# Softmax denominators from pairs of key chunks added by an accumulating DMA, and first expert layers beside the last of layer 1

## The chip, the cores and the metric

The kernel runs on one core of one Trainium2 chip. The metric is the device time of a run in microseconds (us). The engines have short names in the profile: PE is TensorE's products, PEld its weight loads, DVE is VectorE, ACT is ScalarE, POOL is GpSimd and SP is SyncE, which here only issues DMAs. A PSUM tile is a buffer that products are written to; an eviction is the ScalarE instruction that reads such a tile and writes its values elsewhere; a DMA's landing is the moment at which the profile sees it done. The granted clock is the share of full speed that the profile gives for TensorE.

## The reference, cut to what matters

```python
# x: 8 images, 256 channels, 32 x 32 pixels, float32
# layer 0: attention over pooled keys and values, 8 heads of 32, 1426 keys
attn = softmax(einsum('bhqd,bhkd->bhqk', q_g, k) * SCALE)
out_att = einsum('bhqk,bhkd->bhqd', attn, v)
...                                # projection, added to x
# layer 1: attention over tokens, then 8 experts on every token
t = t + attn(_ln_t(t))
h = relu(bn(einsum('bfd,edh->bfeh', x, W1) + b1))
h = relu(bn(einsum('bfeh,ehk->bfek', h, W2) + b2))
y = einsum('bfeh,ehd->bfed', h, Wo) + bo
t = t + einsum('bfed,fe->bfd', y, w)   # w: gates from the mean over all images
```

The gates need all eight images, so the experts' third products cannot start before layer 1 has ended for the last one. Their first two layers need only their own image.

## The kernel before

It has three stages: a start (first image's pooled keys and values), the attention loop of layer 0, and the experts. The loop has 8 images x 2 groups of four heads x 2 halves of the queries x 12 key chunks = 384 steps. A step makes the scores of one chunk, the Exp on ScalarE, and for the chunk before it the values and the denominators; the denominators are products with a matrix of ones:

```python
def scores(b, c, sl, kc):
    t = T(psum, [P, 4, 512], "sc")                 # one buffer
    for j in range(4):                             # four heads, row-tiled
        f.pe.matmul(t[:w, j, :], lhsT=ks[b, c][r, k0 : k0 + w], rhs=qs[b, c][r, sl], ...)
    pt = T(work, [P, 4, 512], "pt", bufs=2)
    f.act.activation(pt[:w], t[:w], AF.Exp, scale=SCALE0)

def values(b, c, kc, pt, pv):
    for what in range(2):                          # 0: values, 1: ones
        for j in range(4):                         # column-tiled
            lhsT = kit.ones[:w, :DH] if what else vts[b][kc // 4][:w, kc % 4, h * DH : (h + 1) * DH]
            f.pe.matmul(pv[DH * j : DH * j + DH, what, :], lhsT=lhsT, rhs=pt[:w, j, :], ...)
```

`f` is a recorder. It keeps a simple clock for each engine, holds a list of background jobs (pooling, statistics, projections, layer 1), puts pieces of them between the steps, and pins every engine's instructions in the order in which it wrote them. The experts of the kernel before do not use it; there, the ordering tool that schedules the rest of the program is free:

```python
def layer(dst, wt, e, src, s, c):                  # one expert layer, 256 -> 256, 512 tokens
    ps = T(psum, [P, 2, 512], "sc")                # two buffers
    for m in range(2):
        for k in range(2):
            nc.tensor.matmul(ps[:, m, :], lhsT=wt[:, e, k, m * P : (m + 1) * P], rhs=src[:, k, :], ...)
    for m in range(2):
        nc.scalar.activation(dst[:, m, :], ps[:, m, :], AF.Relu, bias=col(c, e, m), scale=col(s, e, m))
```

## Time and profile before

The median of three runs is 3865.12 us (3863.69 to 3868.33). The profiled execution, from the timeline of TensorE:

| stage | from, to (us) | length |
|---|---|---|
| start, to the first scores | 0 to 177.9 | 177.9 |
| attention loop, 384 steps | 177.9 to 2281.2 | 2103.3 |
| end of layer 1, gates, experts | 2281.2 to 3859.8 | 1578.6 |

Two rows of the page cut the span into 40 slices of 96 us; a digit is the busy share in tenths, of TensorE and of the 16 DMA engines:

```profile
PE   3499999999899899899899997799999999999999
...
DMA  1010001000010010010000010500000000000000
```

TensorE is full nearly everywhere and the DMA engines are nearly empty. The row of groups for the ones products is (busy us, mean ns of one | idle before them):

```profile
L657 PE MATMUL pv<-pt,con 128*32 128x512 f32 (+1 forms) x3072 | 399.7, 592 | 0.0
```

3072 instructions are two for each of four heads in 384 steps. The other views are shown in the prediction.

### The profile page before, as it was taken

To read this page: it belongs to the slowest core of one execution; us is meant where nothing else is said; L and a number is where in the kernel's file an instruction comes from. 1 tells how busy PE (TensorE), PEld (TensorE's weight loads), DVE (VectorE), ACT (ScalarE), POOL (GpSimd) and SP (SyncE) were. 2 spreads that over 40 slices of the span, in tenths; PEclk is the share of its full clock that TensorE was granted. 3 is DMA by queue.
4 is the path that set the end of the run, shared out by engine and by line. 5 is a ranking of instruction groups with operands and counts; after the bars stand their busy time and mean duration, and the time that the engine had idled before them with its cause. 6 is when DMAs were issued, how large, how long until landed. Compare 5 with 4: busy or idle time off the path is not lost.

```text
span 3859.8 us, 40154 instructions
## 1 busy us (share of the span) xinstructions
PE 3625.5 (94%) x16666; PEld 1624.4 (42%) x16666; DVE 1389.2 (36%) x2533; ACT 1505.2 (39%) x1625; POOL 762.8 (20%) x848
## 2 busy tenths in 40 slices
PE   3499999999899899899899997799999999999999
PEld 1233344434444444444444455444444444444444
DVE  5555563846636626636522121211111111111111
ACT  1256555564454554454454421212222222222222
POOL 3132324324224224224222222100000000000000
PEclk7699999999999999999999998879999999999999
DMA  1010001000010010010000010500000000000000
GB/s 40 14 39 26 15 4 47 12 28 20 12 36 20 12 36 23 9 36 23 9 28 28 17 46 23 195 17 17 17 17 16 22 17 28 16 17 17 17 11 12
DMA packets 55296, 99.97 MB, mean 26 GB/s; under 512 B 6448, under 2 KB 31672, under 8 KB 52928
## 3 DMA queue, kind: packets, MB, share of 16 engines
q1 hardware_dynamic: 49440, 84.76, 6.3%
q0 software_dynamic: 1152, 8.39, 0.5%
q10 hardware_dynamic: 4512, 4.16, 0.3%
q8 instruction: 133, 2.18, 0.2%
q14 instruction: 59, 0.48, 0.0%
HBM read 61.64 MB, written 35.66 MB: 25 GB/s over the span
## 4 chain that ended last, share of the span: by engine, by line
PE 75%; DVE 13%; issue 4%; POOL 4%; ACT 4%; DMA 0%; ACTq 0%; POOLq 0%; DVEq 0%
PE sc L1701 23%; PE sm L657 20%; PE y L1748 12%; PE pv L657 11%; DVE acc L657 10%; PE sc L657 8%; ACT pt L657 3%; DVE rec L657 1%; POOL s L657 1%; POOL bound L657 1%; PE y L1743 1%; PE sc L1807 1%; POOL rstd L657 1%; DVE tst L657 0%; POOL acc L657 0%
## 5 line engine op out<-in xcount | busy, mean ns | idle before, releaser
L657 ACT ACTIVATE pt<-sc 128x2048 f32<-128x2048 f32 (+1 forms) x384 | 720.9, 1877 | 547.4 <-PE sc L657 546.8
L1709 ACT ACTIVATE h<-sc,bnvec 128x512 f32<-128x512 f32 x512 | 370.7, 774 | 1011.9 <-PE sc L1701 977.1
L657 DVE SCALAR_TENSOR_TENSOR acc<-p,vec,acc 128x961 f32<-128x961 f32 (+7 forms) x1024 | 628.9, 623 | 150.0 <-POOL acc L657 119.2
L1733 DVE TENSOR_TENSOR h<-h,gb 128x1024 f32<-128x1024 f32 x128 | 156.9, 1225 | 1116.1 <-ACT h L1709 1095.8
L1701 PE MATMUL sc<-hn,w1e 128*128 128x512 f32 x1024 | 462.0, 594 | 9.4 <-DVE bnvec L1676 9.4
L1748 PE MATMUL y<-h,wo 128*128 128x512 f32 x1024 | 463.6, 597 | 0.0
L1701 PE MATMUL sc<-h,w2e 128*128 128x512 f32 x1024 | 460.2, 592 | 0.0
L657 PE MATMUL sc<-q,kn 32*128 32x512 f32 (+1 forms) x3072 | 438.0, 640 | 13.4 <-ACT pt L657 13.3
L657 PE MATMUL pv<-pt,vt 128*32 128x512 f32 (+1 forms) x3072 | 409.9, 605 | 0.0
L657 PE MATMUL pv<-pt,con 128*32 128x512 f32 (+1 forms) x3072 | 399.7, 592 | 0.0
L1701 PEld LDWEIGHTS sc<-hn,w1e 128*128 128x128 f32 x1024 | 195.3, 191 | 255.0 <-issue 255.0
L1748 PEld LDWEIGHTS y<-h,wo 128*128 128x128 f32 x1024 | 194.3, 191 | 251.9 <-issue 251.7
L1701 PEld LDWEIGHTS sc<-h,w2e 128*128 128x128 f32 x1024 | 194.6, 190 | 244.9 <-issue 244.9
L657 PE MATMUL sm<-p,v 128*128 128x256 f32 x1024 | 245.2, 401 | 40.5 <-DVE rec L657 40.5
L657 ACT ACTIVATE p<-sm 128x512 f32<-128x512 f32 (+1 forms) x224 | 130.7, 584 | 364.5 <-PE sm L657 356.4
L657 PE MATMUL sm<-y,t 128*128 128x256 f32 x1024 | 243.3, 387 | 3.1 <-ACT p L657 2.7
L657 PEld LDWEIGHTS sm<-p,v 128*128 128x128 f32 x1024 | 206.7, 203 | 79.5 <-DVE rec L657 42.1
L657 POOL TENSOR_TENSOR rstd<-rstd,mhalf 128x4 f32<-128x4 f32 (+2 forms) x88 | 84.5, 960 | 749.9 <-DVE rstd L657 749.9
L657 PEld LDWEIGHTS sm<-y,t 128*128 128x128 f32 x1024 | 190.5, 191 | 73.5 <-issue 42.6
L657 PEld LDWEIGHTS pv<-pt,con 128*32 128x32 f32 (+1 forms) x3072 | 99.6, 110 | 230.9 <-issue 230.9
L657 PEld LDWEIGHTS sc<-q,kn 32*128 32x128 f32 (+1 forms) x3072 | 115.0, 176 | 193.7 <-issue 119.8
L657 PE MATMUL sm<-xp,kvw 128*128 128x512 f32 (+1 forms) x384 | 176.8, 601 | 15.1 <-DVE xp L657 6.7
(177 smaller groups left out, 2599.3 us busy)
## 6 DMA issues: line engine op xcount, KB each, us to landing
xp<-in_x_dram SPq DMA_DIRECT2D x8, 1024.0 KB, 5.8
t<-in_x_dram SPq DMA_DIRECT2D x8, 1024.0 KB, 6.8
t<-t SPq DMA_DIRECT2D x8, 1024.0 KB, 3.9
res<-t SPq DMA_DIRECT2D x32, 256.0 KB, 3.3
t<-o SPq DMA_DIRECT2D x32, 256.0 KB, 2.4
hn<-o SPq DMA_DIRECT2D x32, 256.0 KB, 2.7
hn<-hn SPq DMA_DIRECT2D x16, 512.0 KB, 4.0
t<-t SPq DMA_DIRECT2D x16, 512.0 KB, 4.0
```

Of the source, the lines that this page charges most:

```text
L657: ins = fn(*args, **kwargs)
L1701: nc.tensor.matmul(ps[:, m, :], lhsT=wt[:, e, k, m * P : (m + 1) * P], rhs=src[:, k, :], start=k == 0, stop=k == 1,)
L1709: nc.scalar.activation(dst[:, m, :], ps[:, m, :], AF.Relu, bias=col(c, e, m), scale=col(s, e, m))
L1733: nc.vector.tensor_tensor(h, h, gb[:, e : e + 1, sl].to_broadcast([P, 2, 512]), ALU.mult)
L1743: nc.tensor.matmul(y[m], lhsT=bo[:, m * P : (m + 1) * P], rhs=gt[:, sl], start=True, stop=False)
L1748: nc.tensor.matmul(y[m], lhsT=wo[:, e, k, m * P : (m + 1) * P], rhs=h[:, k, :], start=False, stop=e == NE - 1 and k == 1,)
L1807: nc.tensor.matmul(ps[:, sl], lhsT=sel[:, e * P : (e + 1) * P], rhs=gt[:, sl], start=True, stop=True)
```

## The change

It has two intents. First, two neighbouring chunks of Exp are added by a DMA that accumulates into the first of them, and one ones product per pair replaces two. Second, the experts' first two layers are written by the same recorder, so that they run beside layer 1 of the last images, staged through DRAM until the gates are known. Much of the recorder and of the buffers changes with it. The core, cut:

```diff
+        def add(kc, pt, into):
+            w = KEY_CHUNKS[kc][1]
+            f.pool.dma_start(out=into[:w]..., in_=pt[:w]..., accum_op=ALU.add)
+
+        def sums(kc, s, total):
+            for j in range(4):
+                f.pe.matmul(total[DH * j : DH * j + DH, :], lhsT=kit.ones[:, :DH], rhs=s[:, j, :],
+                            start=kc == 1, stop=kc == NKC - 1)
...
-            pt = T(work, [P, 4, 512], "pt", bufs=2)
+            pt = T(work, [P, 4, 512], "pt", bufs=6)
...
+                if kc1 % 2:
+                    add(kc1, pts.pop(i - 1), pts[i - 2])
+                    due.append((i + 4, kc1, pts.pop(i - 2), av, behind))   # sums four steps later
...
+        lag = 3.0 if engine == "SP" else LANDING                  # LANDING = 9.5
...
         def layer(dst, wt, e, src, s, c):
-            ps = T(psum, [P, 2, 512], "sc")
+            ps = T(psum, [P, 2, 512], "layer", bufs=2)
             for m in range(2):
                 for k in range(2):
-                    nc.tensor.matmul(
+                    f.pe.matmul(
...
-            for m in range(2):
-                nc.scalar.activation(dst[:, m, :], ps[:, m, :], AF.Relu, ...)
+                f.act.activation(dst[:, m, :], ps[:, m, :], AF.Relu, ...)
+            f.step(PACE2)
...
+        while not gated and n2 < NSTAGED:      # first layers until the gates are there
+            first(n1)
+            n1 += 1
+            if n1 > 1:
+                second(n2, True)               # staged through DRAM
+                n2 += 1
```

## The prediction

> **What bounds the kernel now.** I read the page's busy slices first, to find the stages, then cut the span at the points that the TensorE timeline gives: the first score product starts at 177.9 us, the last at 2281.2, the experts' first product at 2457.5, and from 2552 on TensorE has no gap. The busy time of these stretches (columns: PE, PEld, DVE, ACT, POOL, each with its instructions, then granted clock, DMA share, GB/s):
>
> ```profile
> 0.00:178.00 178.00, 67.32 (x176) 35.06 (x176) 100.72 (x237) 34.42 (x64) 43.90 (x55) 0.70 0.09 29
> 178.00:2282.00 2104.00, 2041.38 (x12822) 888.83 (x12822) 1049.36 (x2025) 1072.99 (x1012) 663.75 (x734) 0.99 0.07 23
> 2282.00:2457.00 175.00, 125.17 (x468) 89.99 (x464) 41.85 (x90) 18.77 (x28) 48.48 (x51) 0.85 0.14 47
> 2457.00:2552.00 95.00, 90.95 (x202) 40.99 (x203) 28.16 (x28) 31.35 (x41) 6.64 (x9) 0.81 0.44 171
> 2552.00:3852.00 1300.00, 1300.00 (x3006) 569.50 (x3006) 168.44 (x152) 347.69 (x481) 0.00 (x0) 1.00 0.05 17
> ```
>
> In the attention loop (384 steps in 2104 us, 5.48 us each) TensorE works 97% of the time; VectorE and ScalarE are at half. So the loop is TensorE's, with 63 us idle. The last image's layer 1 and the gates (2282 to 2552) leave 54 us idle and run at a clock of 0.85 and 0.81. The experts are pure TensorE at full clock. The start is a chain through VectorE. So TensorE work taken out of the loop counts nearly in full, unless something else ends a step later.
>
> What that would be shows in two neighbouring steps without background work:
>
> ```profile
> 1166.00 1.14 PE L657 MATMUL sc<-q,kn 32*128 32x512 f32 x8 [0.20 <-ACT pt L657]
> ...
> 1167.07 1.06 PE L657 MATMUL pv<-pt,vt 128*32 128x512 f32 x8
> 1167.27 1.88 ACT L657 ACTIVATE pt<-sc 128x2048 f32<-128x2048 f32 x1 [1.32 <-PE sc L657]
> ...
> 1167.96 1.04 PE L657 MATMUL pv<-pt,con 128*32 128x512 f32 x8
> ...
> 1169.24 1.14 PE L657 MATMUL sc<-q,kn 32*128 32x512 f32 x8
> ```
>
> The score tile has one buffer, so the next scores wait for this Exp: 1.27 us from the scores' start to the Exp's, 1.88 of Exp, 0.09 to the next scores, 3.24 us in all (1166.00 to 1169.24). TensorE's own starts lie 1.07 (scores), 0.89 (values) and 0.97 (ones) apart, 2.93 in sum. A step with no background is already bound by ScalarE, by 0.2 to 0.3 us.
>
> What ends TensorE's idle time (total, times, longest):
>
> ```profile
> PE sm L657 <- DVE acc L657: 48.9, 4, 18.3
> PE sm L657 <- DVE rec L657: 40.5, 4, 10.3
> PE sm L657 <- POOL diag L657: 21.4, 7, 4.5
> ...
> PE sc L657 <- ACT pt L657: 13.3, 58, 0.6
> ```
>
> The first is the start; the second is one stall of 10 us per image in the middle of the loop, where the written order runs ahead of VectorE; the third is mostly the layer-1 tail.
>
> **What the Trainium skill says.** "TensorEngine Tiling (Array Packing)", Key Properties: changing the tiling mode drains TensorE. The trace agrees: the column-tiled values take 0.89 us when the ones, in the same tiling, follow, and the ones take 0.97 when a full-array product follows. "DMA: Bandwidth & Descriptors", Anatomy of one DMA, gives about 2.0 us plus bytes/436e3 for a DMA issued by GpSimd: 4.4 us for 1 MB, as an estimate. This trace's nearest thing, a plain 1 MB load issued by GpSimd, takes longer to land:
>
> ```profile
> feat<-hn POOLq DMA_DIRECT2D x7, 1024.0 KB, 8.3
> ```
>
> The same page, SDMA does more than copy, puts the largest count for the adding unit at 2048 elements; a row of one Exp tile is 4 x 512 = 2048, so each row can be one piece. No run here shows an accumulating DMA yet. "SBUF — State Buffer", Who interferes with whom, says a DMA does not contend with compute engines, but that GpSimd's descriptor writing can be shut out by VectorE; the trace has GpSimd issues of 0.53 us, too few to test it.
>
> **The change part by part.**
>
> *Ones products.* 384 groups go, 192 come. A removed group costs 0.88: when it goes, the values before it take its drain. Over the loop the spacing has a median of 0.88 (values before ones) and 0.97 (ones before background). A new group stands alone between background and scores: 0.96; directly after the values 0.88. So 384 x 0.88 - 192 x about 0.94 = 338 - 181 = 157 us less TensorE time. The group's busy time (399.7 us, half of it 200) overstates this, because modelled ends overlap and the drain stays.
>
> *Exp becomes the bound of bare steps.* Without ones a bare step has 1.07 + 0.97 = 2.04 us of TensorE work against the 3.24 us of Exp chain, or 3.0 with a sum group. I took the instruction order of both built kernels, gave each background product its spacing from this trace (0.91 us for 512 columns, 0.46 for 256, 0.13 for a transpose), and added up max(0, 3.24 - step). Before: 22 us in 65 steps (the trace has 13 on PE and some more on its weight loads), and a loop of 2038 us against 2041 measured busy, so the count is sound. After: 62 us in 110 steps. So +40 us.
>
> *Shifted background.* The same count gives 898 us of background in the loop before and 782 after: 117 us of layer 1 move behind the loop. That is neutral in work, and it is what the experts' first layers are to run beside.
>
> *Stalls in the loop.* The order is written by a new recording model: it knows the Exp wait, the shared port and open buffers, and no step now has more than 8 us of background. I let the 50 us of stalls other than Exp fall to 30: -20.
>
> *The tail.* Now the first experts' layers alternate with layer 1, staged through DRAM. Idle 54 us. Slow clock: the work between 2282 and 2552 is 106 (layer 1) + 16 layers x 3.43 = 55 + 19 (gates) = 180 us at full clock, against 216 busy, so 36. Of these 90 us I give back 35: the last pair's DMA (about 9 us, with two sum groups directly behind the last values), then reciprocal 3.35 and multiply before the projection, with only one 4 to 8 us batch in between; about 5 us until the first expert weights land; a few short chains. Net -55.
>
> *Start.* The starting value of each depthwise sum moves from GpSimd to ScalarE (saves about 3 us at the first), but the map buffer becomes single and each map waits for the convolution before it (19.4 us each): three gaps of 5 to 7 us more on VectorE, and query products move out of the last 40 us. Net +8.
>
> *Other engines.* ScalarE gains about 74 us (starting values) and 50 (copies with sums), so some 1150 of 1850 us; VectorE gains about 100 (adds of layer 1, attention multiply), about 62% busy. GpSimd loses its sums and gets 192 issues. None becomes a bound on average.
>
> Sum: -157 + 40 - 20 - 55 + 8 = -184 from 3865: about 3680 us. By stages: 186 + 1850 + 1640 + 4.
>
> **The rivals.**
> 1. *The DMA sets the step.* 192 transfers in 1850 us is one per 9.6 us. An accumulate reads two streams and writes one; the page's fit with 2 MB gives 6.8 us, with 3 MB 9.2, and the measured 8.3 us for a plain load hints at more. The sum comes four steps after the issue, 13 us in bare steps and 19 on average, so a landing of 8 to 11 us is hidden. At 12 us of occupancy each the loop would last 2300 us: total near 4130. Against: the changed kernel's own model takes 9.5 us for landing, chosen, I assume, from a measurement. About one in fifteen.
> 2. *The ones come out in full, the Exp wait is filled.* If the background fills what I counted as waiting and the stalls vanish, the loop is 1742 + 10 and the tail loses 80: total near 3560.
> 3. *More stalls.* Several buffers become single, ScalarE's queue delays Exps behind the new evictions, hardware DMAs land later beside accumulates. If the order runs ahead of VectorE as before and 0.2 us per step are added, the loop is 80 us longer: 3760.
>
> **Range and chances.** Rivals 2 and 3 are shifts of -120 and +80 that partly occur; the range is 3590 to 3755. More than 2% faster means below 3788; only rival 1 or a doubled rival 3 misses it.
>
> **What would show it.** Ones products at half the count with about 0.95 us a group; the scores' waits for Exp at 50 to 80 us instead of 13; sums waiting for DMA close to nothing; accumulating DMAs landing in 8 to 11 us; the first scores at about 186 us, the last at about 2035; clock near 1 between there and the experts. It is wrong if sums wait for the DMA in most steps, or if the loop keeps stalls of 10 us per image.

## The result, and the profile after

The changed kernel takes 4093.26 us (median of four runs, 4084.45 to 4096.98), beside 3865.01 for the kernel before. The ratio is 1.0586 (95% interval 1.0567 to 1.0605): slower. A ratio here is the mean time of one kernel's runs over that of the other's runs in the same rounds, so it is not quite the ratio of the medians quoted. Executions over 1.5% slower than the fastest of the same kernel are left out of the means. The prediction, 3680 with a range to 3755, was wrong in sign. By its own stages:

| stage | before | predicted | after | after less predicted |
|---|---|---|---|---|
| start | 177.9 | 186 | 169.8 | -16 |
| loop | 2103.3 | 1850 | 1981.5 | +132 |
| rest | 1578.6 | 1640 | 1931.3 | +291 |

The slices of the kernel after are 102 us each:

```profile
PE   3587899989999989999997889888888888888888
...
DMA  1165645564555455455455211123332000000000
```

Two things differ from before. The DMA engines are half busy through the whole loop, and TensorE has eights all through the experts, where it had nines. The stretches show it in numbers (columns as in the prediction): the loop, the stretch in which experts and layer 1 alternate, and the experts alone:

```profile
170.00:2152.00 1982.00, 1828.00 (x10779) 736.36 (x10778) 1017.14 (x2061) 1148.41 (x1328) 377.57 (x483) 0.97 0.54 119
...
2198.00:2700.00 502.00, 441.04 (x1424) 255.45 (x1424) 113.23 (x227) 146.64 (x234) 21.79 (x28) 0.98 0.24 85
2700.00:4075.00 1375.00, 1198.51 (x2657) 485.37 (x2656) 175.63 (x159) 305.70 (x393) 0.00 (x0) 1.00 0.13 47
```

In the experts alone TensorE is busy 1199 of 1375 us at full clock, where it had no gap before: 176 us are lost there. The waits of TensorE name the releaser (total us, times, longest):

```profile
PE layer L663 <- ACT h L663: 231.5, 256, 2.0
PE sm L663 <- DVE xr L663: 50.9, 16, 6.8
PE sc L663 <- ACT pt L663: 43.3, 65, 1.9
```

256 waits are exactly one for each expert layer (8 experts x 16 half images x 2 layers), 0.90 us each. The timeline shows what such a layer looks like. The kernel before had eight products and then the two evictions as one block:

```profile
2466.35 3.60 PE L1701 MATMUL sc<-h,w2e 128*128 128x512 f32 x8
2466.55 1.45 ACT L1709 ACTIVATE h<-sc,bnvec 128x512 f32<-128x512 f32 x2 [1.66 <-PE sc L1701]
2469.78 3.60 PE L1701 MATMUL sc<-hn,w1e 128*128 128x512 f32 x8
```

After, each layer stops in the middle:

```profile
3501.70 1.88 PE L663 MATMUL layer<-h,w2e 128*128 128x512 f32 x4
3501.90 0.78 ACT L663 ACTIVATE h<-layer,bnvec 128x512 f32<-128x512 f32 x1 [2.08 <-PE layer L663]
3503.62 0.78 ACT L663 ACTIVATE h<-layer,bnvec 128x512 f32<-128x512 f32 x1 [0.94 <-PE layer L663]
3504.45 1.98 PE L663 MATMUL layer<-h,w2e 128*128 128x512 f32 x4 [0.87 <-ACT h L663]
3506.27 3.60 PE L663 MATMUL y<-h,wo 128*128 128x512 f32 x8
```

The second half of the layer (3504.45) waits for the eviction of the first half (3503.62 + 0.78). A layer takes 2.75 + 1.82 = 4.57 us from its start to the next group's, where it took 3.43. That is 1.14 us more, and 256 x 1.14 = 292 us, beside an excess of 291 in the rest of the kernel. (This is one layer, scaled up; over all recorded layers the median is 4.62 us after and 3.43 before.)

In the loop the parts that the prediction counted came. The ones products are half as many and wait for their DMA hardly at all, and a DMA lands in 7.2 us (median):

```profile
L663 PE MATMUL total<-pt,con 128*32 128x512 f32 x1536 | 208.5, 615 | 9.7 <-DMA pt<-pt 9.6
```

```profile
pt<-pt POOLq DMA_DIRECT2D x160, 1024.0 KB, 7.2
```

To see why the loop is nevertheless 132 us too long I added up TensorE's timeline over the loop: each group of products at the spacing that its kind has where nothing waits (1.07 scores, 0.88 a column-tiled group, plus 0.10 where another tiling follows, 0.45 for 512 columns), the waits that the timeline names, and what remains, which is slow clock and small gaps. Later experiments stand in the same table. The count of work is good to some 10 us: f_no_pairs, x_traffic_only, t_copy_only and u_half_traffic run the same products in the same order, and so do a_evict_after and y_no_add, and yet their counts differ by up to 9.

| kernel | loop | work | waits | remainder |
|---|---|---|---|---|
| before | 2103 | 2022 | 62 | 19 |
| after | 1982 | 1761 | 152 | 69 |
| a_evict_after | 1987 | 1753 | 151 | 82 |
| f_no_pairs | 2004 | 1934 | 42 | 28 |
| x_traffic_only | 2116 | 1934 | 129 | 53 |
| t_copy_only | 2048 | 1925 | 74 | 49 |
| u_half_traffic | 2055 | 1929 | 82 | 44 |
| y_no_add | 1868 | 1745 | 75 | 48 |
| z_landing_5p5 | 1910 | 1725 | 120 | 64 |
| w_nopairs_landing | 1915 | 1877 | 24 | 15 |

The work fell by 261 us, near the predicted 157 + 117 = 274. But the waits rose by 90, of which Exp, by the names of the waits, is only 30 (13 to 43), and the remainder by 50. Against the prediction's 1850, stalls other than Exp are 80 us too many (60 more where 20 fewer were expected), the remainder 50, the missing part of the work 13, and Exp 10 too few.

### The profile page after: what moved, and what is told of

It is laid out like the page before. It is cut to its first block, busy times and chain, and to the rows that moved or that the text cites. A ratio compares the mean times of both kernels' runs of the same rounds, so it can differ in the third digit from the quotient of the medians.

```text
span 4082.6 us, 37798 instructions
## 1 busy us (share of the span) xinstructions
PE 3558.1 (87%) x15130; PEld 1525.1 (37%) x15130; DVE 1419.7 (35%) x2701; ACT 1651.0 (40%) x2050; POOL 422.1 (10%) x552
## 5 line engine op out<-in xcount | busy, mean ns | idle before, releaser
L663 ACT ACTIVATE h<-layer,bnvec 128x512 f32<-128x512 f32 x512 | 398.2, 778 | 1323.5 <-PE layer L663 1290.7
L663 DVE SCALAR_TENSOR_TENSOR acc<-p,vec,acc 128x961 f32<-128x961 f32 (+7 forms) x1024 | 571.6, 566 | 165.0 <-ACT acc L663 134.4
L663 PE MATMUL layer<-hn,w1e 128*128 128x512 f32 x1024 | 501.2, 612 | 135.4 <-ACT h L663 118.7
L663 PE MATMUL layer<-h,w2e 128*128 128x512 f32 x1024 | 495.4, 606 | 112.8 <-ACT h L663 112.8
L663 DVE TENSOR_TENSOR h<-h,gates 128x1024 f32<-128x1024 f32 x128 | 156.8, 1225 | 1186.9 <-ACT h L663 814.2
L663 PEld LDWEIGHTS layer<-hn,w1e 128*128 128x128 f32 x1024 | 184.4, 191 | 421.9 <-ACT h L663 225.4
L663 PEld LDWEIGHTS layer<-h,w2e 128*128 128x128 f32 x1024 | 183.4, 190 | 397.2 <-ACT h L663 218.8
L663 POOL DMA_DIRECT2D pt<-pt x192 | 168.8, 879 | 1098.1 <-ACT pt L663 1053.5
L663 PE MATMUL total<-pt,con 128*32 128x512 f32 x1536 | 208.5, 615 | 9.7 <-DMA pt<-pt 9.6
L663 PEld LDWEIGHTS sm<-p,v 128*128 128x128 f32 x1024 | 194.3, 192 | 47.9 <-issue 17.9
L663 POOL TENSOR_TENSOR rstd<-rstd,mhalf 128x4 f32<-128x4 f32 (+2 forms) x88 | 90.2, 1024 | 1016.0 <-DVE rstd L663 788.1
```

The lines of the kernel that those rows point to most:

```text
L663: ins = fn(*args, **kwargs)
```

## The experiments

Each call to the chip ran up to four kernels beside the kernel before, whose median was 3862.08, 3863.78, 3864.16, 3863.53 and 3864.69 us in the five calls, each on another chip. I give the median of four runs and the ratio to the kernel before.

### The experts: what makes each layer wait

Theory 1 was that the eviction inside the loop makes the wait. Its rival was the rest of the change to the tail: the staging through DRAM or the smaller buffers.

**a_evict_after.** Both evictions after all the products of the layer, as in the kernel before:

```diff
                         stop=k == 1,
                     )
-                f.act.activation(dst[:, m, :], ps[:, m, :], ...)
+            for m in range(2):
+                f.act.activation(dst[:, m, :], ps[:, m, :], ...)
```

> The changed kernel with one edit: in each expert layer both halves' products are issued before the two evictions, as in the kernel before. Theory 1 (one PSUM tile per layer: the second half's products wait for the first half's eviction, 2.75 + 1.82 = 4.57 us a layer where 3.43 is free, 256 layers): 292 us less, about 3800 us, and TensorE's wait on the expert eviction (231.5 us) gone. Theory 2 (the staging of h2 through DRAM or the smaller buffers slow the experts): stays at 4080 to 4095.

Measured: 3802.72 us, ratio 0.9834 (0.9812 to 0.9856). One moved line is worth 290 us. The layer is a block again:

```profile
3303.47 3.60 PE L663 MATMUL layer<-hn,w1e 128*128 128x512 f32 x8
3306.91 3.60 PE L663 MATMUL layer<-h,w2e 128*128 128x512 f32 x8
```

The rest after the loop is now 3802.1 - 2157.2 = 1645 us; the prediction said 1640.

**b_two_tiles.** The eviction stays inside the loop, but each half has a PSUM tile of its own:

```diff
-            ps = T(psum, [P, 2, 512], "layer", bufs=2)
             for m in range(2):
+                ps = T(psum, [P, 512], "layer", bufs=4)
```

> The changed kernel with the eviction left between the halves, but each half in a PSUM tile of its own (four of one bank in place of two of two banks). Theory 1 says that the tile, not the order of the evictions, makes the wait: about 3800 us like the first run, or a few us less because evictions start earlier. If the order alone did it: stays near 4090. Theory 2: stays near 4090.

Measured: 3794.59 us, ratio 0.9828 (0.9808 to 0.9848). So it is not the place of the eviction by itself but the shared tile: the second half's products write a tile that an eviction is reading, and the tool makes them wait, though they write other columns. The chip does not ask for that here. The Trainium skill, "PSUM — Partial Sum Buffer", Summary: rules for kernel authors, says to aim reads of PSUM at a different bank than the running product's; by the same page a bank is 512 float32 values, so the two halves of the tile are different banks. This run agrees: with the same halves as two tiles the profile names no wait of a layer for an eviction any more, and the result is correct.

**d_before_inloop.** The reverse test: the kernel before with its eviction moved into the loop.

```diff
-            for m in range(2):
-                nc.scalar.activation(dst[:, m, :], ps[:, m, :], ...)
+                nc.scalar.activation(dst[:, m, :], ps[:, m, :], ...)
```

> The kernel before with one edit: the eviction of each half moved between the halves' products, as the changed kernel has it. Theory 1: 256 layers x 1.14 us = 292 us more, about 4157 us. Theory 2: unchanged, 3865 us.

Measured: 3943.1 us, ratio 1.0209 (1.0192 to 1.0226): 81 us more, not some 290. The expectation failed. The timeline shows why:

```profile
3300.64 1.02 PE L1701 MATMUL sc<-h,w2e 128*128 128x512 f32 x2
3301.50 1.02 PE L1747 MATMUL y<-h,wo 128*128 128x512 f32 x2
3302.53 1.98 PE L1701 MATMUL sc<-h,w2e 128*128 128x512 f32 x4
```

In the kernel before the order of the experts is not pinned, and the ordering tool puts other products (here of the third layer) between the halves, so that much of the eviction is hidden. The mended theory: the shared tile makes the wait, and the recorder's fixed order leaves nothing to fill it.

**e_before_pinned.** d_before_inloop, with the experts' products and evictions issued through the recorder, which pins their order:

```diff
+    f = Flow(tc, kit)
-                    nc.tensor.matmul(
+                    f.pe.matmul(
-                nc.scalar.activation(dst[:, m, :], ...)
+                f.act.activation(dst[:, m, :], ...)
```

> The kernel before with the eviction between the halves and, in addition, the experts' products and evictions issued through the recording layer, which fixes the program order. Run d cost only 81 us, because the tool that orders the program there moved another product between the halves (the trace of d shows second-layer and output products between them). Theory 1 in its mended form (the wait costs 1.14 us a layer only where the order is fixed): 292 us more than before, about 4155 us, with a wait on the eviction about 256 times. Rival (the wait is always mostly filled and something else of the changed experts cost the 290): near 3943 like d.

Measured: 4161.74 us, ratio 1.0772 (1.0754 to 1.079): 298 us over the kernel before, and TensorE waits for an eviction 255 times, 232.5 us in all. The mended theory holds. That pinning alone could be the cost is ruled out by a_evict_after: its experts are pinned too, and its layers take 3.43 us.

**g_no_overlap.** a_evict_after with layer 1 ended before the experts begin:

```diff
+        f.finish(lambda: ended[0] == nb)
         last(f, (l1, shared), ended)
```

> Run a's kernel with layer 1 finished before the experts start. The prediction gave the overlap 90 us of idle time and slow clock, less 35: layer 1 has about 230 us of work behind the loop here instead of 111, so its chain-bound gaps double: 80 to 150 us more than run a, 3885 to 3950, with a clock of about 0.85 in that stretch. Rival (the overlap only moves idle time): within 30 us of 3803.

Measured: 3911.18 us, ratio 1.0118 (1.0101 to 1.0135). Running the experts' first layers beside layer 1 is worth 108 us in the mended kernel. That part of the change does what it was made for.

### The loop: single buffers?

**c_xr_stage.** TensorE's second largest wait is for the sum of projection and residual (`xr`), which has one buffer. In this run the residual takes turns with another tile:

```diff
-                    xt = T(work, [P, 512], "xr")
+                    xt = T(work, [P, 512], ("xr", "stage")[half])
```

> The first run's kernel, and the residual tiles of the projection take turns in two buffers (the second is the one that stages queries) instead of one. In the changed kernel VectorE waits 169 us for the residual's load, because that load must wait for the store of the quarter before, and TensorE waits 51 us (16 times) for the small PSUM tile that VectorE then frees late[...]. Theory: 60 to 100 us less than the first run, about 3720. Rival (VectorE's convolutions, not the load, hold it): within 15 us of the first run.

Measured: 3810.86 us, ratio 0.9859 (0.9842 to 0.9875), against 3802.72 without it. No gain: in the loop TensorE's waits for `xr` fell from 46 to 14 us, but waits for `stage`, now filled by VectorE as well as ScalarE, came to 31 and 18. A second buffer of its own did not fit beside six probability buffers.

**h_lag3_xr2_p2.** To make room the pairs' sums come three steps after the DMA in place of four, with five probability buffers; the residual and the map of the depthwise sums (`p`) get two buffers each, and the condition under which the next map starts is loosened by one:

```diff
-    due.append((i + 4, kc1, ...
+    due.append((i + 3, kc1, ...
-    xt = T(work, [P, 512], "xr")
+    xt = T(work, [P, 512], "xr", bufs=2)
...                                       # pt bufs 6 to 5, p bufs 1 to 2
```

> Run a's kernel with the sum three steps after its DMA instead of four, so that five Exp tiles do instead of six; the 8 KB a partition go to second buffers for the depthwise map and the projection's residual. Theory (the six Exp tiles forced other tiles single, and that is the loop's 109 us of stalls besides Exp, with about 50 us of slow clock after them): 50 to 110 us less than run a, 3690 to 3750, and sums wait for the DMA under 25 us in all, as it lands 7.2 us after its issue. Rival (the written order is what stalls): within 20 us of 3803, as run c was. If the landing needs four steps: slower than run a.

Measured: 3800.09 us, ratio 0.9833 (0.9816 to 0.9849). No gain either. SyncE's waits for the store of the residual, 86 us in a_evict_after, are gone, yet TensorE's waits for `xr` stay at 43 us (46 before): the loads themselves now land in 3.9 us in the median, where they took 2.7 in a_evict_after. So these two single buffers are not what holds the loop back.

### The loop: what the pairs are worth

**f_no_pairs.** a_evict_after without pairs and without the accumulating DMA: one ones product per chunk, directly behind its values.

```diff
-                if kc1 % 2:
-                    add(kc1, pts.pop(i - 1), pts[i - 2])
-                    due.append((i + 4, kc1, pts.pop(i - 2), av, behind))
+                if kc1 == 0:
+                    total = T(psum, [P, 512], "total")
+                sums(kc1, pts.pop(i - 1), total)
...
```

> Run a's kernel without the pairs: one ones product per key chunk directly after its values, no accumulating DMA, all buffers as in run a. By the count of the prediction the pairs are worth 157 us of TensorE less 40 of new waits for Exp: 117 us, so about 3920 us. If the DMAs or the waits ate it (rival: pairs are worth nothing on the chip), it stays within 30 us of 3803. If the loop's other stalls (109 us in the changed kernel) are filled when TensorE has more to do, 30 to 100 us: 3830 to 3900.

Measured: 3788.17 us, ratio 0.9802 (0.9786 to 0.9818). The pairs, from which the prediction had taken 157 - 40 = 117 us, are worth -15. In the table the loop of f_no_pairs has 181 us more work than that of a_evict_after, but 109 us less waiting and 54 less remainder. It is thus 17 us longer; the rest of the kernel is 32 us shorter, in part because more of layer 1 ran inside the loop (68 more products of 256 columns and 8 of 512, some 19 us). The recorder also wrote another order, so the next two runs hold the order fixed. (The traces confirm it: the products, and VectorE's and ScalarE's instructions, come in the same order in x_traffic_only as in f_no_pairs, and in y_no_add as in a_evict_after.)

**x_traffic_only.** The traffic without the saving: f_no_pairs with the 192 accumulating DMAs issued after both chunks have been read, kept out of the recorder's clock so that the order stays.

```diff
-                sums(kc1, pts.pop(i - 1), total)
+                sums(kc1, pts[i - 1], total)
+                if kc1 % 2:
+                    add(kc1, pts.pop(i - 1), pts.pop(i - 2))   # nothing reads the sum
```

> f_no_pairs with the 192 accumulating DMAs still issued, each after both of its chunks have been read by their own ones products, so that nothing uses their sum: the traffic without the saving. The order of the instructions on every engine is that of f_no_pairs, but for the added DMA issues on GpSimd. Contention theory (beside accumulating DMAs the plain DMAs land later, so VectorE's residual statistics and with them TensorE come late): the 15 us that the pairs lose were a saving of some 160 us of products less some 175 us of waits, slow clock and other losses, so the time rises from 3788 to 3870 to 3930, and the loop's waits from 42 to over 120 us. Rival (the waits of a_evict_after come from its other order, which the recorder chose by its model of the landings): no waits are added, the time stays within 15 us of 3788.

**y_no_add.** The saving without the traffic: a_evict_after with the DMA left out and only the recorder's note of it kept. Its output is wrong, which doesn't matter for the time.

```diff
-            f.pool.dma_start(out=into[:w]..., in_=pt[:w]..., accum_op=ALU.add)
+            f.note("POOL", "dma_start", None, (), dict(out=into[:w]..., in_=pt[:w]...))
```

> a_evict_after with its 192 accumulating DMAs left out, everything else issued in just the same order; the ones products then sum only every second chunk, so the result is WRONG ON PURPOSE (denominators about half). The saving without the traffic. Contention theory: the waits of the loop fall from 151 to about 50 us and the time from 3803 to 3650 to 3720. Rival (the recorder's order makes the waits): the time stays within 15 us of 3800.

Measured: x_traffic_only 3909.9 us (ratio 1.0133, 1.0102 to 1.0165), 122 us over f_no_pairs. y_no_add 3680.88 us (ratio 0.9524, 0.9508 to 0.954), 122 us under a_evict_after. (The program's test of y_no_add found its output correct within tolerance all the same.) The two agree on what the traffic costs, and y_no_add against f_no_pairs gives an idea of what the saving is worth alone: 107 us, near the predicted 117. These two differ in their order as well, and an order alone can be worth 29 us (w_nopairs_landing below), so the 107 is not exact. TensorE's waits in the loop, first of f_no_pairs:

```profile
PE sc L663 <- ACT pt L663: 15.5, 24, 1.5
...
PE sm L663 <- DVE xr L663: 3.5, 3, 2.3
```

and of x_traffic_only, in the same order of instructions:

```profile
PE sm L663 <- DVE xr L663: 48.1, 13, 9.7
```

Taking the traffic away from a_evict_after does the reverse. The same wait in a_evict_after and in y_no_add, both up to 2170 us:

```profile
PE sm L663 <- DVE xr L663: 46.2, 14, 6.9
...
PE sm L663 <- DVE xr L663: 5.9, 4, 3.4
```

That stretch takes in 130 us behind the loop of y_no_add; inside its loop the wait is 2.5 us.

VectorE's `xr` is the projection plus the residual; the residual comes by a DMA. Medians of issue to landing in f_no_pairs:

```profile
q<-hn SPq DMA_DIRECT2D x14, 512.0 KB, 3.9
...
t<-xr SPq DMA_DIRECT2D x28, 256.0 KB, 2.4
```

and in x_traffic_only:

```profile
pt<-pt POOLq DMA_DIRECT2D x152, 1024.0 KB, 7.3
q<-hn SPq DMA_DIRECT2D x14, 512.0 KB, 5.0
...
t<-xr SPq DMA_DIRECT2D x28, 256.0 KB, 4.0
```

The median of the residual's own load hardly moves (2.6 and 2.7 us). But the store of one residual (`t<-xr`) must land before the next is loaded into the same tile. SyncE's own waits for that store (total, times, longest) are in f_no_pairs:

```profile
SPq L663 <- DMA t<-xr: 45.1, 22, 2.7
```

and in x_traffic_only:

```profile
SPq L663 <- DMA t<-xr: 102.2, 22, 10.5
```

The longest is four times as long, and as SyncE's order is pinned, the DMAs written behind the wait are issued late too. VectorE's wait for the loaded residual grows with it, from 86 us in all (longest 6.0) to 174 (longest 17.5). So the largest path reads: accumulates run beside the plain DMAs, these land late, VectorE's sum is late, and TensorE, in its pinned order, stands. At TensorE's longest such wait (9.7 us) the load was issued at 1525.0 and landed at 1531.5, VectorE's sum began at 1531.7, and TensorE went on at 1532.5. Of the loop's 112 us between the two runs, 87 are waits of TensorE; 45 of them are for `xr`, 14 for other DMAs directly and 9 for Exp. The remainder, 25, goes with a mean granted clock of 0.97 in place of 0.99. That GpSimd's issuing slows VectorE is not seen: VectorE is busy 1019 us in the one loop and 1024 in the other.

**z_landing_5p5.** The recorder takes 3.0 us for the landing of a plain DMA. This run tells it 5.5:

```diff
-            lag = 3.0 if engine == "SP" else LANDING
+            lag = 5.5 if engine == "SP" else LANDING
```

> a_evict_after with one number of the recorder's model changed: it takes 5.5 us instead of 3.0 us for the landing of a plain DMA of SyncE, near what the trace shows beside the accumulates (medians 3.9 to 6.6 us). If the contention costs time only because the order was made for landings of 3 us, the work that needs them is now put later, the waits of VectorE on DMAs stop reaching TensorE and the time falls from 3803 to 3690 to 3740. If the landings delay a chain that has no slack whatever the order, the time stays within 20 us of 3803.

Measured: 3768.84 us, ratio 0.9756 (0.974 to 0.9772), 34 us less than a_evict_after and short of what was expected if misjudged landings were the whole cause. TensorE's waits for `xr` fall from 46 to 9 us, but all its waits in the loop only from 151 to 120.

**r_best.** f_no_pairs with two PSUM tiles per layer, and second buffers for the residual and the depthwise map (the expectation calls it weight preparation) in the memory that the pairs had taken (probability buffers 6 to 3).

```diff
-            ps = T(psum, [P, 2, 512], "layer", bufs=2)
             for m in range(2):
+                ps = T(psum, [P, 512], "layer", bufs=4)
...
-            pt = T(work, [P, 4, 512], "pt", bufs=6)
+            pt = T(work, [P, 4, 512], "pt", bufs=3)
-                    xt = T(work, [P, 512], "xr")
+                    xt = T(work, [P, 512], "xr", bufs=2)
-                p = T(work, [P, NK], "p")
+                p = T(work, [P, NK], "p", bufs=2)
```

> f_no_pairs (no pairs) with a PSUM tile for each half of a layer, and the memory of the dropped pairs given to second buffers: probability buffers 6 to 3, residual tile 1 to 2, weight-preparation row 1 to 2. The best version that the runs point to. From f_no_pairs 3788 and the 8 us between a_evict_after and b_two_tiles I expect 3780; if the single residual buffer does hold back something where the landings are short, 3750 to 3770; if three probability buffers are too few, up to 3810.

Measured: 3784.74 us, ratio 0.9795 (0.9778 to 0.9811): within 4 us of f_no_pairs. Again extra buffers bring nothing.

### What of the traffic costs, and can the sum be had otherwise

**t_copy_only.** x_traffic_only with plain copies in place of the accumulates:

```diff
-                out=into[:w]..., in_=pt[:w]..., accum_op=ALU.add
+                out=into[:w]..., in_=pt[:w]...
```

> x_traffic_only with the 192 DMAs as plain copies (the addition left out), into buffers that nothing reads any more; correct result, same order of instructions. If the addition itself makes these DMAs heavy, they land sooner than 7.3 us, take well under 41 % of the DMA engines' time, and the time falls from 3910 to 3790 to 3830. If moving 1 MB each is what costs, the landing stays near 7 us and the time within 20 us of 3910.

Measured: 3844.58 us, ratio 0.9953 (0.9937 to 0.997). It lies between the two expectations: moving the bytes costs 56 us over f_no_pairs, and accumulating another 65. Landing and share of the DMA engines' time in the loop:

```profile
q0 software_dynamic: 23952, 168.16, 22.7%
...
pt<-pt POOLq DMA_DIRECT2D x156, 1024.0 KB, 4.7
```

In x_traffic_only the same queue took 41.1% and a DMA 7.3 us. The addition nearly doubles the time that a DMA holds the engines.

**u_half_traffic.** Every second accumulate of x_traffic_only left out.

```diff
                 if kc1 % 2:
-                    add(kc1, pts.pop(i - 1), pts.pop(i - 2))
+                    one, two = pts.pop(i - 1), pts.pop(i - 2)
+                    if kc1 % 4 == 1:
+                        add(kc1, one, two)
```

> x_traffic_only with every second of the accumulating DMAs left out (96 in place of 192); correct result, same order of instructions. In proportion: about 61 us over f_no_pairs, 3850 (3830 to 3865). If only DMAs close to one another hurt (queues that build up), less: 3790 to 3820. If a single one in the way is enough to spoil the chain that has no slack, more: 3870 to 3910.

Measured: 3848.42 us, ratio 0.9967 (0.9948 to 0.9985): 60 us over f_no_pairs for half of the DMAs. Half of the accumulates cost half. Their queue's share in the loop:

```profile
q0 software_dynamic: 13392, 97.52, 24.3%
```

That is 24.3% for 60 us, beside 22.7% in t_copy_only for 56 and 41.1% in x_traffic_only for 122. So the cost goes with the time that these DMAs hold the DMA engines, and not with the number of issues by GpSimd: 96 here and 192 in t_copy_only cost the same.

**s_vector_adds and s_gpsimd_adds.** a_evict_after with the pair added by VectorE, or by GpSimd:

```diff
-            f.pool.dma_start(out=into[:w]..., in_=pt[:w]..., accum_op=ALU.add)
+            f.ve.tensor_tensor(into[:w], into[:w], pt[:w], ALU.add)      # or f.pool
```

> a_evict_after with the pairs added by VectorE in place of the accumulating DMA (one tensor_tensor of 128 x 2048 each, some 4 x 0.69 = 2.8 us by the trace's 0.69 us for 128 x 512; 192 of them, some 500 us more on an engine that is busy 1017 of the loop's 2000 us). Correct result. If only the DMA's traffic ate the saving: 3690 to 3730, near y_no_add's 3681 with some waits for VectorE. If VectorE's queue becomes the wait in its place (adds of 2.8 us ahead of the statistics): 3780 to 3850, with TensorE's waits for VectorE above those of a_evict_after.

> The same with GpSimd adding: an engine busy 377 us of the loop, of which the issues of the DMAs (0.88 us each, some 170 us) fall away; by the recorder's model an addition takes 4.9 us, 192 of them 940 us. If only the traffic ate the saving and GpSimd does not hold VectorE up: 3690 to 3740. If GpSimd's additions hold up VectorE's work or their own consumers (GpSimd's small operations of the gate wait behind them): above 3780.

Measured: 3869.76 us (ratio 1.0014, 0.9997 to 1.0031) and 4114.99 us (ratio 1.0647, 1.0629 to 1.0665). The DMA traffic is gone, and a worse wait takes its place. With VectorE adding, its largest new group is:

```profile
L663 DVE TENSOR_TENSOR pt<-pt,pt 128x2048 f32<-128x2048 f32 x160 | 369.5, 2311 | 50.3 <-ACT pt L663 50.3
```

VectorE's run is slower than even the worse of its two expectations (3780 to 3850). VectorE's busy time in the loop's first 1979 us goes from 1010 to 1405. That leaves it free time, but its chains (statistics of the keys, then ScalarE's normalised keys) come late, and TensorE's waits for those keys are 85 us where a_evict_after had 8. With GpSimd adding, the group is:

```profile
L663 POOL TENSOR_TENSOR pt<-pt,pt 128x2048 f32<-128x2048 f32 x160 | 742.6, 4643 | 719.0 <-ACT pt L663 688.3 <-PE sm L663 30.7
```

and VectorE's depthwise sums, which nobody touched, take 894 ns each in that stretch where they took 566, beside GpSimd's additions of 4.6 us.

**w_nopairs_landing and v_two_landing.** The control for z_landing_5p5: f_no_pairs with the same 5.5 us. And the pairs with both repairs: z_landing_5p5 with two PSUM tiles. Both change the one line of z_landing_5p5; the second also has the edit of b_two_tiles:

```diff
-            lag = 3.0 if engine == "SP" else LANDING
+            lag = 5.5 if engine == "SP" else LANDING
```

> f_no_pairs (no accumulating DMAs) with the assumed landing of SyncE's plain DMAs at 5.5 us in place of 3.0 us. If the 34 us of z_landing_5p5 come from late landings beside the accumulates, there is nothing to gain here: 3788 within 12 us, or a little slower. If the later order is better anyhow: 3745 to 3765.

> z_landing_5p5 with a PSUM tile for each half of a layer (b_two_tiles). From 3769 and the 8 us between a_evict_after and b_two_tiles: 3761 (3750 to 3775), which would be the fastest correct version of the study.

Measured: 3759.0 us (3755.34 to 3761.63; ratio 0.9732, 0.9716 to 0.9748) and 3763.58 us (3757.72 to 3772.32; ratio 0.9745, 0.9726 to 0.9763). The first expectation failed in an instructive way: without any accumulates the longer assumed landing gains 29 us, nearly the 34 that it gained with them. So that gain is not about the contention: the order written for later landings is better here with and without accumulates, and z_landing_5p5 is no evidence for the contention theory. What carries that theory is x_traffic_only and y_no_add, with t_copy_only and u_half_traffic. Both kernels beat the one before and the change; they are too close to call between them. The pairs are worth nothing measurable in this order too.

## Why the prediction was wrong, and where it was right

**The rest of the kernel: the step that failed is "The experts are pure TensorE at full clock", with a tail of 1640 us.** That was true of the kernel before, and I carried it over. The diff moves the eviction into the loop over halves, where both halves share a tile, and the experts go over to the recorder, which pins the order. I counted the products, with "16 layers x 3.43" from the old trace, and never followed one layer through its tile. A layer takes 4.57 us. It cost 1.14 us in each of 256 layers, 292 us. The repair alone (a_evict_after) gives 290 back, and two tiles do it as well; the same fault put into the kernel before costs 298 if the order is pinned and 81 if not. With the repair the rest takes 1645 us: the tail's own sum was right.

**The loop: the step that failed is "I let the 50 us of stalls other than Exp fall to 30: -20".** They rose by 60, and the remainder by 50. The stalls that the prediction had in view did go, but it misread them: "one stall of 10 us per image" are four in all for eight images, as its own line says (40.5 us, 4 times). Others came in their place. I had the mechanism in hand as part of rival 3 ("hardware DMAs land later beside accumulates") and gave it, with two other causes, at most 80 us; with the order held fixed it costs 122. Taking the traffic away brings the loop's waits from 151 to 75 and the remainder from 82 to 48, so it makes most of both rises; the loop of y_no_add takes 1868 us where 1850 were predicted. For rival 1 I asked only whether the accumulating DMA itself lands in time. That it does: TensorE's ones products wait 9.6 us for it in all. I did not ask whom it delays. The Trainium skill, "DMA: Bandwidth & Descriptors", Issuing engines are not separate DMA queues, says that DMAs started by any engine end up on the same 16 DMA engines and interleave. The runs agree: `t<-xr`, issued by SyncE, goes from 2.4 to 4.0 us beside GpSimd's accumulates. The section that I did cite, on DMA not contending with compute engines, was no answer to that question.

**The ones products were right and the Exp waits nearly so.** Half as many groups; TensorE's waits for Exp are 43 us, a little below the "50 to 80"; the net of both, 117 predicted, is about 107 when the traffic is left out (y_no_add against f_no_pairs, in two orders). The 117 us of layer 1 shifted behind the loop came about too: work in the loop fell by 261 against 274.

**The landing** was 7.2 us, sooner than the "8 to 11", and sums waiting for DMA "close to nothing" held. **The start** was predicted 8 us longer and is 8 shorter; no run looked at it alone.

By stages: -16 at the start, +132 in the loop and +291 after it make 407 of the 413 us between 3680 and 4093; the rest lies between the profiled span and the median. With the repaired layers and without the traffic (y_no_add, wrong result) the kernel takes 3681 us, just the number predicted; that it is so close is luck, as the start was 16 us shorter and the loop 18 longer.

What stays open: which of the plain DMAs costs most. The residual's chain is the largest wait and the clearest, but giving its tile company (c_xr_stage) or a second buffer (h_lag3_xr2_p2) did not help; that other late transfers stand close behind it is likely, but no run shows it. Nor was it shown whether the slower clock in the loop is only a consequence of the waits.

## What to carry to other kernels

When a change moves instructions under a recorder that fixes their order, follow one instance of each rewritten helper through its tiles: here the program's waits kept an eviction and the next product on one tile apart, though they touch different halves, and the fixed order did not fill the gap. When work goes from TensorE to DMA engines, ask not only whether the transfer lands in time but which other transfers it delays, and who waits for those. A saving and its side effect can be measured apart, in one order of instructions, by running the traffic without the saving and the saving without the traffic.

## What the Trainium skill lacked or had wrong

- "DMA: Bandwidth & Descriptors", Anatomy of one DMA: its fit makes an estimate of 4.4 us for a 1 MB copy issued by GpSimd, and the plain copies between SBUF tiles landed in 4.7 (t_copy_only), so it fits. For accumulating DMAs between SBUF tiles the page has no figure: they took 7.3 us (x_traffic_only), and 41.1% of the DMA engines' time in the loop where the copies took 22.7%, at one DMA per about 11 us.
- "DMA: Bandwidth & Descriptors", Issuing engines are not separate DMA queues: it says that DMAs interleave, not what that costs. Here a 256 KB store went from 2.4 to 4.0 us in the median, SyncE's longest wait for one from 2.7 to 10.5 us, and the kernel lost 122 us although the DMA engines were only half busy.
- "PSUM — Partial Sum Buffer": it tells which banks may be read beside a running product; no page says that two halves of one tile in different banks are still kept apart in time by the program's own waits. That cost 1.14 us a layer (after), and nothing with two tiles (b_two_tiles).
- "SBUF — State Buffer", Who interferes with whom: its rule fits (a VectorE instruction with two SBUF inputs contends with a GpSimd instruction that reads SBUF), but it has no figure for this pair of operations. Depthwise sums of 566 ns took 894 beside GpSimd additions of 4.6 us (s_gpsimd_adds).
